# Masks of the decision trees by DMA in half of the blocks, and DRAM fills as planned steps, in a twelve-layer decoder kernel

## The chip, the cores and the metric

The kernel runs on one core of one Trainium2 chip. The metric is the device time of one execution in microseconds; the median of three runs of the kernel before is 2126.63 us (2123.84 to 2128.03).

## What is computed

64 sequences of 64 tokens, 128 wide, pass through four decoder layers of three sublayers each; every sublayer reads the layer norm of `x` and adds its result to `x`. The reference, cut to what matters here:

```python
x = x + _L0_attn_ref(_layernorm(x), ...)            # differential attention
x = x + _L0_xattn_ref(ctx_1024, _layernorm(x))      # alignment (dynamic time warping) with ctx
x = x + _L0_ffn_ref(_layernorm(x), ...)             # three trees (q, k, v), then attention over them
x = x + _L1_attn_ref(...); x = x + _L1_xattn_ref(...); x = x + _L1_ffn_ref(...)   # the last: experts
x = x + _L2_attn_ref(...); x = x + _L2_xattn_ref(...); x = x + _L2_ffn_ref(...)
x = x + _L3_attn_ref(...); x = x + _L3_xattn_ref(...); x = x + _L3_ffn_ref(...)   # the last: experts
# each tree of L0_ffn:
for _ in range(DEPTH):                              # 4 levels, 16 leaves
    score = jnp.einsum('nd,nd->n', xf, node_w[cur]) + node_b[cur]
    cur = 2 * cur + 1 + (score >= 0)
sel = jax.nn.one_hot(cur - N_NODES, N_LEAVES)
hidden_all = jax.nn.relu(jnp.einsum('nd,ldh->lnh', xf, w1) + b1[:, None, :])      # 64 wide per leaf
hidden = hidden_all * sel.T[:, :, None]
out = jnp.einsum('lnh,lho->no', hidden, w2) + sel @ b2
```

All leaves are computed for all tokens, and those that a token did not choose are masked.

## The kernel before

The 4096 tokens are 8 blocks of 512 (`NB`, `BT`), four tiles of 128 tokens each; `x` stays in SBUF for the whole run.

**Order of the work.** The program has five stages: a setup, the first flow (`front_group`: L0, L1 up to the router of its experts), the pages of L1's experts (`L1_ffn`), the last flow (`L2_group`: L2 and L3 up to the router), and L3's experts (`L3_ffn`). In a flow, every step is given to a planner (`Flow.add`) with its engine and a cost in microseconds, the steps that it follows, the buffers that it takes and frees, and a `tail`: the time after its end until its result counts as there (a DMA's landing). `Flow.play` plays the steps on a model of the five engines and the buffer rings: always the one that can begin first, ties by rank, which is a number of its group (layer and block) less the longest way that is left behind it. `ORDERS` holds these numbers for the two flows, one for each group in the order in which the groups are added; if the count fits, they are the start, and 300 variations of them are played. The best play's order is then emitted, and each engine runs its instructions in just that order. SP (SyncE) issues all plain DMAs of the flows, in order, as one queue. Instructions of the setup lie outside that order: the framework places them by their dependencies and their place in the program.

**The setup** loads `x`, the constants and the weights of L0's attention. `run` (L2594 on) clears a zero tile `z`, a part of `r`, the table of the alignment (`dt_r`). `setup_L3_ffn` (L2483, L2484) writes it to the 8 experts' ranges of `moe_x` and to the spare rows of the output, `setup_L1_ffn` (L2111) to 8 ranges of `pages`: 17 fills of DRAM, 660 KB most of them. `open_L0_ffn` (L1691, L1693) loads the trees' two matrices, q, k and v, 512 KB each; then follow 23 small loads (L1046, L1701).

**First flow.** L0's attention runs block by block; DVE takes each score's maximum (L546) and subtracts it (L555). The alignment works on two halves of the blocks (`ALIGN`: 0 to 3, 4 to 7): each block's distances (`L0_dist`: its load `ld` of ctx at L1476 and L1478, squares on ACT at L1483), then for all four blocks a root, a store to DRAM, a border written into `r` (`bd`, POOL), a load back (L1562), a chain of 64 row scans on DVE (L1571), masks, and 64 scans backwards (L1633); a store, and per block a product with ctx (L1671). The trees of a block (`flow_L0_ffn`) wait for that.

**The trees.** For each of three trees `m` and four pairs `pr` of two leaves' columns: an up step (`u`, PE), two matmuls with `w1` (L1770) and two with a leaf table `f0_em` (L1772) that add -2^100 to the columns of leaves not chosen, taken from `notT` (one less the transposed choice); a ReLU with the bias (`r`), on ACT (L1781) or DVE (L1783), which makes the masked columns zero; a down step (`d`, PE) with `w2` (L1797, or L1807 for the third tree), at the last pair also with `b2` and the choice. The two PSUM pairs `mm`, three `hT` buffers (ring H) and two places `dnq` limit how many steps are open. The ring G has 18 buffers of 2 KB per partition for nearly everything else.

**Where things meet.** A router (`f1`, `f3`) norms `x` (`norm_parts`, with `hold` for steps to wait for), chooses experts and scatters rows by GpSimd (L894). In the last flow, a step `("out", blk)` stores `x` to the output before the router norms it in place.

Of the kernel before, what the change touches and what calls it, by code (L numbers as in the profile page):

```python
# [13 lines left out]
F32 = mybir.dt.float32  # L14
# [24 lines left out]
    "G": (512, "xn xT qT kT o oT sq sqT sT cn cT d2 iv mn up selT qk va f0e f0p rxT x1hn x1hid x1hT x1qT x1s x1pT x1ht x1z ycT yk yv yw "  # L39
# [3 lines left out]
    "A": (1024, "a2g"), "nT": (BT // 2, "nT"),  # L43
# [9 lines left out]
            mk=3, pb=1, nT=2, sel=2, dnq=2, H=3, f0b=3)  # L53

ALIGN = (((0, 1, 2, 3), 0), ((4, 5, 6, 7), 64))
CH = 8
# [11 lines left out]
        -78, -130, -17, 83, 425, 288, 115, 418, -33, 78, -134, -156, 215, -90, 682, 1069,  # L68
        303, 144, -1217, 183, 789, -13, 984, 583, 481, 437, 284, 311, -1038, 373, 195, 674,
        712, 393, 386, 668, -42, 541, 336, 716, 395, 991, 806, 438, 608, 426, 954, 7,  # L70
        1467, 1071, 1229, 1113, 735, 436, 169, 809, 1278, -142, 384, -48, 197, -359, -463, -65,
        1393, 119, 168,
    ),
    "last": (
        73, 34, 202, 80, 99, 97, 99, 104, 237, 223, 166, 253, 232, 275, 304, 249,
        120, -51, 133, 224, 273, 279, 293, 300, 182, 260, 272, 280, 460, 443, 297, 421,
        240, 294, 248, 291, 283, 227, 312, 426, 324, 285, 380, 385, 224, 524, 526, 513,
        428, 588, 339, 442, 724, 441, 631, 469, 499, 576, 363, 568, 530, 473, 594, 609,
# [949 lines left out]
class Decoder:  # L1028
    def __init__(self, ctx, tc, ins, out):
        self.tc, self.nc, self.ins, self.out = tc, tc.nc, ins, out  # L1030
        self.base = self.const = ctx.enter_context(tc.tile_pool(name="const", bufs=1))
        self.small = ctx.enter_context(tc.tile_pool(name="small", bufs=4))
        self.dram = ctx.enter_context(tc.tile_pool(name="scratch", bufs=1, space=DRAM))
        self.psum = ctx.enter_context(tc.tile_pool(name="psum", bufs=1, space=PSUM))
        self.now, self.owed, self.turns = {}, {}, {"ps": 0, "mm": 0}
        self.flip = 0
        self.route1 = None
        self.half = None

# [202 lines left out]
    def loaded(self, fl):  # L1242

        key = ("loads", 0, "in")
        if key not in fl.keys:
            fl.add(key, {"SP": .1}, lambda e: None, tail=80.0)
        return key

    def front_group(self, layers):

        with ExitStack() as ctx:
# [4 lines left out]
            def parts(pools_ctx, pools, fl):  # L1256
                x = [None] * NB
                if "L0_ffn" in layers:
                    self.open_L0_ffn(pools_ctx)
# [12 lines left out]
                if "L0_ffn" in layers:  # L1272
                    x = [self.flow_L0_ffn(fl, blk, x[blk]) for blk in range(NB)]
# [15 lines left out]
                if r is not None:  # L1289
                    for blk in range(NB):  # L1290
                        r.flow(fl, blk, x[blk], hold=self.aligned)
                    self.flow_shared(fl, r)
# [3 lines left out]
            self.attend(parts, G=18, B=6, lg=1, rt=1)  # L1296
# [163 lines left out]
    def flow_L0_xattn(self, fl, blks, p0, x):  # L1460
# [98 lines left out]
        add("bd", {"POOL": .5}, border, [("L0_dist", blks[-1], "bn")])  # L1559
# [125 lines left out]
    def open_L0_ffn(self, ctx):  # L1685
        nc, ins = self.nc, self.ins
        one = self.f0 = self.pool(ctx, "f0", 1)
        self.f0_w1 = one.tile([P, 3, 8, P], F32, name="w1")
        self.f0_w2 = one.tile([P, 3, 8, D], F32, name="w2")
        for m, k in enumerate("qkv"):  # L1690
            nc.sync.dma_start(self.f0_w1[:, m].rearrange("p c f -> p (c f)").rearrange("p (l h) -> p l h", h=64),  # L1691
                              ins[f"L0_ffn_{k}_w1"].rearrange("l d h -> d l h"))
            nc.sync.dma_start(self.f0_w2[:, m], ins[f"L0_ffn_{k}_w2"].rearrange("(c p) o -> p c o", p=P))  # L1693
        self.f0_b1 = self.load("f0_b1", ins["L0_ffn_b1T"], [P, 3, 8], pool=one)
        self.f0_nw = self.load("f0_nw", ins["L0_ffn_node_wT"], [P, 45], pool=one)
        self.f0_nb = self.load("f0_nb", ins["L0_ffn_node_b"].partition_broadcast(P), [P, 45], pool=one)
        self.f0_em = self.load("f0_em", ins["c_leaf"], [96, 8, P], BF16, pool=one)
        self.f0_b2 = one.tile([96, D], F32, name="b2")
        nc.gpsimd.memset(self.f0_b2, 0.0)
        for m, k in enumerate("qkv"):  # L1700
            nc.sync.dma_start(self.f0_b2[32 * m : 32 * m + 16, :], ins[f"L0_ffn_{k}_b2"])  # L1701
        self.f0_sel = [one.tile([P, TB, 3, 32], F32, name=f"sel{i}") for i in range(2)]
        for t in self.f0_sel:
            nc.gpsimd.memset(t, 0.0)

    def flow_L0_ffn(self, fl, blk, x):
        nc, one, c = self.nc, self.f0, self.c
        w1, w2, em, b2 = self.f0_w1, self.f0_w2, self.f0_em, self.f0_b2
# [43 lines left out]
        def leaves_out(e):  # L1752
            tp = self.flat(st.pop("tp"))[:96]
            st["selT"] = self.sb("selT")[:96]
            st["notT"] = self.sb("nT", (P, BT), BF16)[:96]
            if e is nc.scalar:
                nc.scalar.copy(st["selT"], tp)
                nc.scalar.activation(st["notT"], tp, AF.Identity, bias=self.ones[:96, 0:1], scale=-1.0)
            else:
                nc.vector.tensor_copy(st["selT"], tp)  # L1760
                nc.vector.tensor_scalar(st["notT"], tp, -1.0, 1.0, ALU.mult, ALU.add)

        def up(m, pr):
            k = slice(32 * m, 32 * m + 16)

            def f(e):
                st["hT", m, pr] = self.sb("hT", (P, 2, BT))
                ps = st["up", m, pr] = self.pair()
                for i in range(2):
                    nc.tensor.matmul(ps[:, i], w1[:, m, 2 * pr + i, :], st["xT"], start=True, stop=False)  # L1770
                for i in range(2):
                    nc.tensor.matmul(ps[:, i], em[k, 2 * pr + i, :], st["notT"][k], start=False, stop=True)  # L1772
            return f

        def relu(m, pr):
            def f(e):
                ps, hT = st.pop(("up", m, pr)), st["hT", m, pr]
                for i in range(2):
                    b = self.f0_b1[:, m, 2 * pr + i : 2 * pr + i + 1]
                    if e is nc.scalar:  # L1780
                        nc.scalar.activation(hT[:, i], ps[:, i], AF.Relu, bias=b)  # L1781
                    else:
                        nc.vector.tensor_scalar(hT[:, i], ps[:, i], b, 0.0, ALU.add, ALU.max)  # L1783
            return f

        def down(m, pr):
            k = slice(32 * m, 32 * m + 16)

            def f(e):
# [3 lines left out]
                ps, hT = st["dn", m], st.pop(("hT", m, pr))  # L1793
                last = pr == 3
# [5 lines left out]
                else:  # L1800
                    if pr == 0:

                        nc.tensor.matmul(ps, self.onesb[0:1, :], em[0:1, 1:5, :].rearrange("p c f -> p (c f)"), start=True, stop=False)
# [60 lines left out]
        add("lv", {"PE": .55}, leaves, ["dc"], [("tp", "lv", 1), ("selT", "selT", 3), ("nT", "nT", 12)], [("sel", "sel")])  # L1864
        add("lo", {"ACT": 1.15, "DVE": 1.35}, leaves_out, ["lv"], [], [("tp", "lv")])
        for m in range(3):
            for pr in range(4):
                add(f"u{m}{pr}", {"PE": 2.35}, up(m, pr), ["xT", "lo"] + ([f"u{m}{pr-1}"] if pr else []), [("mm", f"u{m}{pr}", 1), ("hT", f"h{m}{pr}", 1)] + ([] if pr else [("dnq", f"d{m}", 1)]),
                    [("xT", "xT"), ("nT", "nT")])
                add(f"r{m}{pr}", {"ACT": 1.4, "DVE": 1.5}, relu(m, pr), [f"u{m}{pr}"], [], [("mm", f"u{m}{pr}")])  # L1870
                add(f"d{m}{pr}", {"PE": 1.75 + (pr == 3) * (.86 if m < 2 else .5)}, down(m, pr),
                    [f"r{m}{pr}"] + ([f"d{m}{pr-1}"] if pr else []),
# [231 lines left out]
    def setup_L1_ffn(self):  # L2104
# [3 lines left out]
        for i in range(0, PAGES, CAP // PAGE):  # L2108
            rows = slice(i * PAGE, min(i + CAP // PAGE, PAGES) * PAGE)
            n = (rows.stop - rows.start) // P  # L2110
            self.nc.sync.dma_start(self.pages[rows, :].rearrange("(t p) d -> p t d", p=P), self.zero[:, 0:n])  # L2111
# [365 lines left out]
    def setup_L3_ffn(self):  # L2477


        self.xg = self.dram.tile([NE * CAP + 2 * NT * P, XROW], F32, name="moe_x")  # L2480
        z = self.zero
        for e in range(NE):
            self.nc.sync.dma_start(self.xg[e * CAP : (e + 1) * CAP, :].rearrange("(c p) d -> p c d", p=P), z)  # L2483
        self.nc.sync.dma_start(self.out[NSEQ * S :, :].rearrange("(c p) d -> p c d", p=P), z[:, :, 0:D])  # L2484

    def L2_group(self, layers):

        with ExitStack() as ctx:
# [10 lines left out]
            def parts(pools_ctx, pools, fl):  # L2499
# [18 lines left out]
                if r is not None:  # L2518
                    for blk in range(NB):
                        fl.add(("out", blk), {"SP": .1}, (lambda b: lambda e: self.nc.sync.dma_start(outb[b], self.x[b]))(blk), [x[blk]])  # L2520
# [254 lines left out]
```

## Time and profile before

| | before |
|---|---|
| median of 3 runs | 2126.63 us |
| the profiled execution | 2125.41 us |
| its span, first to last instruction | 2123.6 us |
| granted TensorE clock, mean | 0.912 |
| busy: PE, PEld, DVE, ACT, POOL | 1834, 1245, 1293, 1078, 880 us |
| first flow: first alignment, first tree matmul (L1770), last | 181 to 288, 317.9, 899 us |
| pages of L1's experts | from about 1085 to 1247 us |
| last flow, then L3's experts | from about 1250, from about 1927 us |

In lists of groups a row gives line, engine, operation, output and input, shapes and count, then busy us and the mean ns of one, then the idle time before them and what ended it. A row of the waits gives the total in us, the times and the longest. In timelines a row gives the start, the time, the engine and the line; `SPq` is the issue of a DMA by SP's queue. A row of the DMA view gives the KB of one and the median us from issue to landing. An f32 matmul shows as two records.

### The profile page before, as it was taken

The numbers are of one execution on the slowest core, as the hardware profiler recorded it, in microseconds if no ns is written. First come the engines' busy times: TensorE is split into PE (matmuls) and PEld (weight loads), VectorE is DVE, ScalarE is ACT, GpSimd is POOL, SyncE is SP. The second block draws the span as 40 slices with busy tenths as digits, with TensorE's granted clock in tenths as the row PEclk, the third lists the DMA queues.
The fourth block names the chain that finished last, engine by engine and source line by source line (L and its number), as shares of the span: only waits on it lengthen the run. The fifth ranks groups of instructions, "written<-read, shape, count | busy, mean of one in ns | idle before, by whom it ended". The sixth has DMA issues, their size and how long they took to land.

```text
span 2123.6 us, 42731 instructions
## 1 busy us (share of the span) xinstructions
PE 1834.1 (86%) x16748; PEld 1245.1 (59%) x16748; DVE 1293.3 (61%) x3683; ACT 1078.0 (51%) x2129; POOL 879.6 (41%) x1196
## 2 busy tenths in 40 slices
PE   7488559999999999998999966899999978936994
PEld 5366344453765554575778854567777756634763
DVE  7488982687574443388324336988988858751211
ACT  7386333443564533477234424776787755622431
POOL 8461215100232334024612247855463364255776
PEclk9798769999999999998899976999999978857998
DMA  9405410101010000010246631100000010024543
GB/s 256 114 22 158 140 46 21 22 20 23 8 37 11 11 21 21 1 50 27 80 116 208 209 109 55 36 21 17 26 22 7 22 56 21 13 66 89 93 68 29
DMA packets 160875, 125.97 MB, mean 59 GB/s; under 512 B 39057, under 2 KB 138690, under 8 KB 160674
## 3 DMA queue, kind: packets, MB, share of 16 engines
q1 hardware_dynamic: 137394, 82.04, 14.2%
q0 software_dynamic: 23280, 41.19, 7.8%
q8 instruction: 133, 2.18, 0.4%
q14 instruction: 68, 0.56, 0.1%
HBM read 75.40 MB, written 45.02 MB: 57 GB/s over the span
## 4 chain that ended last, share of the span: by engine, by line
PE 37%; POOL 10%; DVE 7%; issue 3%; ACT 3%; DMA 2%; SPq 0%; POOLq 0%; ACTq 0%; DVEq 0%
PE ps L1122 5%; POOL out_x L2582 4%; PE ps L590 4%; PE ps L2211 3%; PE mm L2203 3%; PE mm L525 2%; POOL moe_x L894 2%; PE mm L1770 2%; PE ps L2147 2%; POOL A L2273 1%; PE ps L415 1%; PE ps L1797 1%; PE mm L2438 1%; PE mm L2136 1%; PE mm L531 1%
## 5 line engine op out<-in xcount | busy, mean ns | idle before, releaser
L1122 PE MATMUL ps<-cpack,B 128*128 128x128 f32 x1280 | 184.7, 292 | 39.2 <-ACT G L428 25.1
L546 DVE TENSOR_REDUCE e<-mm 128x16 f32<-128x1024 f32 x160 | 191.7, 1218 | 35.8 <-PE mm L525 34.5
L576 ACT COPY B<-ps 128x512 f32<-128x512 f32 x320 | 171.4, 592 | 76.0 <-PE ps L1122 75.3
L1122 PEld LDWEIGHTS ps<-cpack,B 128*128 128x128 f32 x1280 | 153.9, 150 | 87.8 <-issue 26.4
L560 ACT ACTIVATE B<-B 128x1024 f32<-128x1024 f32 x160 | 166.3, 1057 | 67.6 <-DVE B L555 66.4
L1781 ACT ACTIVATE H<-mm,f_b 128x512 f32<-128x512 f32 x166 | 105.0, 683 | 176.3 <-PE mm L1772 174.8
L1132 POOL TENSOR_SCALAR rs_t<-ln_mv 128x4 f32<-128x4 f32 x88 | 19.2, 219 | 412.9 <-DVE ln_mv L1203 389.6
L590 PEld LDWEIGHTS ps<-vx,B 128*64 128x64 f32 x5120 | 167.4, 143 | 38.4 <-issue 12.1
L555 DVE TENSOR_TENSOR B<-mm,e 128x1024 f32<-128x1024 f32 x160 | 189.1, 1213 | 0.0
L1770 PE MATMUL mm<-G,w 128*128 128x512 f32 x384 | 185.4, 605 | 0.0
L590 PE MATMUL ps<-vx,B 128*64 128x18 f32 (+1 forms) x5120 | 179.6, 218 | 2.8 <-ACT B L576 1.1
L1122 PE MATMUL ps<-cpack,G 128*128 128x128 f32 x544 | 96.6, 301 | 82.6 <-ACT G L1223 36.8
L2582 POOL DMA_INDIRECT out_x<-ye,to x80 | 125.1, 1564 | 51.8 <-DVE ye L2580 27.5
L1122 PEld LDWEIGHTS ps<-cpack,G 128*128 128x128 f32 x544 | 66.6, 149 | 121.3 <-ACT G L1223 46.0
L525 PE MATMUL mm<-K,G 32*64 32x256 f32 x2560 | 104.9, 419 | 25.7 <-DVE B L555 23.8
L1223 ACT ACTIVATE G<-x,ln_sh,ln_rs 128x128 f32<-128x128 f32 x208 | 85.7, 487 | 71.9 <-POOL ln_sh L1217 71.9
L2204 ACT ACTIVATE hT<-mm,w 128x256 f32<-128x256 f32 x156 | 68.8, 474 | 104.3 <-PE mm L2203 104.3
L1797 PE MATMUL ps<-H,w 128*128 128x512 f32 x256 | 121.2, 607 | 0.0
L1770 PEld LDWEIGHTS mm<-G,w 128*128 128x128 f32 x384 | 66.7, 190 | 71.4 <-issue 69.8
L2570 ACT ACTIVATE hT<-mm,f_b 128x512 f32<-128x512 f32 (+1 forms) x96 | 58.9, 616 | 83.8 <-PE mm L2569 83.2
L1133 POOL TENSOR_TENSOR ln_rs<-rs_t,neghalf 128x4 f32<-128x4 f32 x88 | 92.9, 1056 | 7.2
L2576 PEld LDWEIGHTS ps<-w,hT 128*128 128x128 f32 x640 | 81.4, 191 | 18.8 <-issue 13.4
(423 smaller groups left out, 4004.1 us busy)
## 6 DMA issues: line engine op xcount, KB each, us to landing
ahead_L_xattn_k<-G SPq DMA_DIRECT2D x24, 256.0 KB, 2.7
moe_x<-r SPq DMA_DIRECT2D x8, 660.0 KB, 9.4
xe<-moe_x SPq DMA_DIRECT2D x8, 660.0 KB, 5.1
xe<-pages SPq DMA_DIRECT2D x39, 132.0 KB, 2.4
paged<-ye SPq DMA_DIRECT2D x39, 128.0 KB, 1.9
pages<-r SPq DMA_DIRECT2D x7, 660.0 KB, 10.6
G<-in_ctx SPq DMA_DIRECT2D x16, 256.0 KB, 3.0
G<-in_ctxT SPq DMA_DIRECT2D x16, 256.0 KB, 3.7
```

The source lines that it names most:

```text
L525: nc.tensor.matmul(banks[g][b * S : (b + 1) * S, pr * 256 : (pr + 1) * 256], qT[rows, at : at + S], kx[rows, :, at : at + S], start=plain ...
L546: nc.vector.tensor_reduce(mx, sc.rearrange("p g (r k) -> p (g r) k", k=S), AX.X, ALU.max)
L555: nc.vector.tensor_tensor(ex, sv, d.bc(st["mx", u].unsqueeze(2), [P, 16, S]), ALU.subtract)
L560: nc.scalar.activation(st["ex", u], st["ex", u], AF.Exp)
L576: (nc.scalar.copy if e is nc.scalar else nc.vector.tensor_copy)(st["pT", u][:, gi], st.pop(("pt", u, gi)))
L590: nc.tensor.matmul(av[b * S : (b + 1) * S, pr, 2 * gi + jp], pT[:, gi, 2 * pr + jp, b * S : (b + 1) * S], v[:, (2 * dp + pr) * 2 + b, 2 * ...
L1122: self.nc.tensor.transpose(t[:cols, i, :], src[:, i, :], self.ident)
L1133: self.nc.gpsimd.tensor_tensor(dst, t, self.neghalf[:, :n], ALU.pow)
L1770: nc.tensor.matmul(ps[:, i], w1[:, m, 2 * pr + i, :], st["xT"], start=True, stop=False)
L1781: nc.scalar.activation(hT[:, i], ps[:, i], AF.Relu, bias=b)
L1797: nc.tensor.matmul(ps, w2[:, m, 2 * pr + i, :], hT[:, i], start=(pr + i == 0), stop=False)
L2582: d = nc.gpsimd.indirect_dma_start(self.out[:, :], bass.IndirectOffsetOnAxis(ap=to[:, r0 + i : r0 + i + 1], axis=0), ye[:, r0 + i, :], Non ...
```

## The change

1. The 17 fills are no longer issued by the setup but are collected in `self.fills`, and become steps `("fill", 0, i)` of the first flow, 3.6 us of SP each; the alignment's border and L1's router wait for all of them. The trees' matrices become three steps `("L0_trees", m, "w")`, 5.6 us of SP each. The other loads count as there 45 us after the start of the plan, not 80.
2. In blocks 4 to 7 (`FOLD`) the up step has no mask matmuls. The transposed choice is also written as bf16 and stored to DRAM (`put`); for each pair two DMAs load the rows of its leaves, each repeated over 64 partitions (`masks`), into one of two buffers of a new ring `fm`, a load being allowed once the up step two before is done (`AHEAD`). The ReLU is one DVE operation, `max(ps, -b1) * mask`, which leaves out the bias; what is missing, `b1 @ w2` of the chosen leaf, is computed once by a small product (`flow_L0_bias`) and added to `b2`.
3. The ring G has 17 buffers in the first flow.
4. In the last flow the store of `x` has a tail of 4.4 us.
5. `ORDERS`: 72 new numbers for the first flow (67 before), 12 of 64 changed in the last.

```diff
+AHEAD = 2
+FOLD = ((False,) * 3,) * 4 + ((True,) * 3,) * 4
...
-            fl.add(key, {"SP": .1}, lambda e: None, tail=80.0)
+            fl.add(key, {"SP": .1}, lambda e: None, tail=45.0)
...
-                        r.flow(fl, blk, x[blk], hold=self.aligned)
+                        r.flow(fl, blk, x[blk], hold=self.aligned + self.filled)
...
-            self.attend(parts, G=18, B=6, lg=1, rt=1)
+            self.attend(parts, G=17, B=6, lg=1, rt=1)
...
-        add("bd", {"POOL": .5}, border, [("L0_dist", blks[-1], "bn")])
+        add("bd", {"POOL": .5}, border, [("L0_dist", blks[-1], "bn")] + self.filled)
...
+            fl.add(("L0_trees", m, "w"), {"SP": 5.6}, weights, tail=2.4)
...
+        add("B", {"POOL": 3.0}, spread, [self.loaded(fl)] + [("L0_trees", m, "w") for m in range(3)], [("f0B", "B", 1)])
+        add("pr", {"PE": 3.0}, product, ["B"], [("tp", "ps", 1)], [("f0B", "B")])
+        add("b2", {"DVE": .5}, plus, ["pr"], [], [("tp", "ps")])
...
+        def put(e):
+            nc.sync.dma_start(rows, st.pop("leaf"))
+
+        def masks(m, pr):
+
+            def f(e):
+                t = st["mask", m, pr] = self.sb("f0m", (P, 2, BT), BF16)
+                at = 32 * m + 4 * pr
+                src = rows[at : at + 4].rearrange("(i h) t -> h i t", h=2)
+                for h in range(2):
+                    nc.sync.dma_start(t[h * S : (h + 1) * S], src[h].partition_broadcast(S))
+            return f
...
-                    nc.tensor.matmul(ps[:, i], w1[:, m, 2 * pr + i, :], st["xT"], start=True, stop=False)
-                for i in range(2):
-                    nc.tensor.matmul(ps[:, i], em[k, 2 * pr + i, :], st["notT"][k], start=False, stop=True)
+                    nc.tensor.matmul(ps[:, i], w1[:, m, 2 * pr + i, :], st["xT"], start=True, stop=fold[m])
+                for i in range(0 if fold[m] else 2):
+                    nc.tensor.matmul(ps[:, i], self.f0_em[k, 2 * pr + i, :], st["notT"][k], start=False, stop=True)
...
+                    nc.vector.scalar_tensor_tensor(hT[:, i], ps[:, i], self.f0_nb1[:, m, ch : ch + 1], st["mask", m, pr][:, i], ALU.max, ALU.mult)
...
+        if any(fold):
+            add("st", {"SP": .7}, put, ["lo"], [], [("f0l", "leaf")], tail=2.6)
...
+                was = order.index(n) - AHEAD if fold[m] else -1
+                if fold[m]:
+                    add(f"k{m}{pr}", {"SP": 1.3}, masks(m, pr), ["st"] + ([f"u{order[was] // 4}{order[was] % 4}"] if was >= 0 else []),
+                        [("f0m", f"k{m}{pr}", 1)], tail=3.0)
...
-            self.nc.sync.dma_start(self.pages[rows, :].rearrange("(t p) d -> p t d", p=P), self.zero[:, 0:n])
+            self.fills.append((self.pages[i * PAGE : min(i + CAP // PAGE, PAGES) * PAGE, :], XROW))
+
+    def flow_fills(self, fl):
+
+        self.filled = []
+        for i, (rows, n) in enumerate(self.fills):
+            c = rows.shape[0] // P
+            f = lambda e, rows=rows, n=n, c=c: self.nc.sync.dma_start(rows.rearrange("(c p) d -> p c d", p=P), self.zero[:, 0:c, 0:n])
+            fl.add(("fill", 0, i), {"SP": 3.6}, f)
+            self.filled.append(("fill", 0, i))
...
-            self.nc.sync.dma_start(self.xg[e * CAP : (e + 1) * CAP, :].rearrange("(c p) d -> p c d", p=P), z)
-        self.nc.sync.dma_start(self.out[NSEQ * S :, :].rearrange("(c p) d -> p c d", p=P), z[:, :, 0:D])
+            self.fills.append((self.xg[e * CAP : (e + 1) * CAP, :], XROW))
+        self.fills.append((self.out[NSEQ * S :, :], D))
...
-                        fl.add(("out", blk), {"SP": .1}, (lambda b: lambda e: self.nc.sync.dma_start(outb[b], self.x[b]))(blk), [x[blk]])
+                        fl.add(("out", blk), {"SP": .1}, (lambda b: lambda e: self.nc.sync.dma_start(outb[b], self.x[b]))(blk), [x[blk]], tail=4.4)
```

## The prediction

> **What bounds the kernel now.** I read the table of windows first, because the program is a row of stages with different limits.
>
> ```profile
> core 0: us, PE busy (x) PEld busy (x) DVE busy (x) ACT busy (x) POOL busy (x), PEclk, DMA share, GB/s
> 0.00:50.00 50.00, 36.63 (x527) 25.41 (x528) 37.20 (x114) 37.08 (x64) 40.82 (x82) 1.00 1.03 256
> 50.00:100.00 50.00, 22.66 (x308) 17.47 (x308) 21.19 (x40) 18.79 (x44) 22.21 (x18) 0.72 0.55 136
> ...
> 200.00:250.00 50.00, 35.15 (x500) 21.20 (x496) 45.16 (x152) 22.67 (x36) 5.37 (x6) 0.88 0.57 199
> 250.00:300.00 50.00, 17.69 (x195) 12.97 (x196) 43.90 (x149) 11.70 (x26) 7.07 (x9) 0.53 0.15 36
> ...
> 350.00:400.00 50.00, 50.00 (x279) 28.57 (x278) 22.09 (x64) 22.68 (x50) 11.70 (x19) 1.00 0.03 8
> ...
> 800.00:850.00 50.00, 50.00 (x198) 24.98 (x197) 16.38 (x74) 17.66 (x37) 22.12 (x32) 1.00 0.07 23
> ```
>
> The columns are busy us (and counts) of PE, PEld, DVE, ACT and POOL. Three things: in 50 to 100 every engine is idle more than half the time, just behind 50 us in which the DMA engines are full; to 318 DVE is the busiest engine (247.7 us against PE's 212.6: attention, then the first alignment); from 300 to 950 PE is busy 644.4 of 650 us, and it is the bound. Then I asked who waited in 40 to 200, and what SP's queue issued there.
>
> ```profile
> ACT G L1483 <- DMA G<-in_ctx: 26.5, 1, 26.5
> PE ps L1122 <- ACT G L428: 25.1, 1, 25.1
> DVE bqs L332 <- DMA L_attn_bq_c<-in_L_attn_bq: 13.5, 1, 13.5
> ```
>
> ```profile
> 14.61 16.85 SPq L2483 DMA_DIRECT2D moe_x<-r  x8
> 31.50 2.35 SPq L2484 DMA_DIRECT2D out_x<-r  x1
> 33.89 20.48 SPq L2111 DMA_DIRECT2D pages<-r  x8
> ...
> 70.77 0.43 SPq L1046 DMA_DIRECT2D L_attn_bk_c<-in_L_attn_bk  x1
> ...
> 76.90 0.39 SPq L1476 DMA_DIRECT2D G<-in_ctx  x1
> ```
>
> SP issues in order. The 17 fills hold it for 39.7 us (16.85 + 2.35 + 20.48), the trees' matrices to 65.9, and 23 small loads (0.47 each) to 76.8; the first load of ctx comes at 76.9. ACT's squares (L1483) wait for it, ACT's later work (L428) is queued behind, and PE stands from 58.3 to 83.4. DVE loses 13.5 and 12.5 us there. As DVE's work up to the end of the alignment (288) decides when the trees' matmuls can begin, these 25 us move everything behind them.
>
> The third look is PE's timeline in the trees:
>
> ```profile
> 800.63 1.88 PE L1770 MATMUL mm<-G,w 128*128 128x512 f32 x4
> 802.44 0.60 PE L1772 MATMUL mm<-nT,f_em 16*128 16x512 bf16 x2
> 802.97 1.98 PE L1770 MATMUL mm<-G,w 128*128 128x512 f32 x4
> 804.89 0.60 PE L1772 MATMUL mm<-nT,f_em 16*128 16x512 bf16 x2
> ```
>
> The mask's two matmuls hold PE for 0.53 us (802.44 to 802.97) of each up step.
>
> **The change part by part, against the profiled execution (2125.41 us, span 2123.6; the median of three is 2126.63, 1.2 more).**
>
> *Fills and tree matrices become planned steps.* Nothing is removed: the same 17 fills and 6 matrix loads pass through SP, but behind the 23 small loads, and between planned ctx loads. The bq load, issued at 70.4 before, should come by about 20 (10.6 + 23 x 0.47 = 21.5), so DVE's 13.5 us wait ends. Ctx loads now stand among the fills: the planner lets SP take a fill of 3.6 us whenever it is free, so by ranks two of the first four blocks' ctx loads pass some fills and two come last. Real fills take 39.7 / 17 = 2.3 us, but start at about 24 (21.5 and one matrix pair), and a load behind them lands as late as they do (9.4 us, row below). After one matrix pair and 8 fills the planner is at 5.6 + 8 x 3.6 = 34 and has ctx at 38; the chip is at 24 + 8 x 2.3 = 42 and has it at 52, while ACT, some 7 us behind the plan (x is there at 6.6), wants it at 45. That is 7 us of a new wait of the same kind, 9 with the load's second half, and 0 if other work stands ahead; as ACT runs in order I take 6. Gain: 25.1 - 6 = 19 (16 to 25). The border (POOL, `bd`) now waits for the fills, and the layer norms' roots are queued behind it on POOL; but the fills end near 70, and the alignment's load was issued at 172.9. The trees' matrices are wanted after 270. If DVE had cover for the wait, the gain would be nothing; its idle 13.5 and 12.5 us say it has none.
>
> *Masks by DMA in blocks 4 to 7.* PE loses 48 x 0.53 = 25.4 us in the stage it bounds. It gains 24 small products for the bias (as L1807: 32 records in 3.84 us are 16 products, so 0.24 each): 5.8 us, or nothing if they fall into PE's gaps before 290 (21.7 and 17.8 us long); I take 2. ReLU of these blocks is now one DVE operation, max and multiply; the nearest row has the same shape, PSUM source and kind:
>
> ```profile
> L2364 DVE SCALAR_TENSOR_TENSOR G<-ps,cpack,Q 128x512 f32<-128x512 f32 x16 | 11.9, 742 | 4.9 <-PE ps L2360 4.8
> L1781 ACT ACTIVATE H<-mm,f_b 128x512 f32<-128x512 f32 x166 | 105.0, 683 | 176.3 <-PE mm L1772 174.8 <-issue 1.3
> ```
>
> 96 x 0.742 = 71 us on DVE, where half of the old 26 (0.746 each, 10 us) go away; ACT loses some 57 us, which gains nothing, since it waits 175 us for PE here. DVE is busy 217 of 400 us in 550 to 950; with 61 more it is at 70%, so PE's other blocks cover it; where a ReLU stands behind a pair of attention reductions (2.4 us) PE may wait: bounds 0 and 12, I take 3.
>
> The mask loads: 96 of 128 KB, 0.62 us of SP each. Nearest rows:
>
> ```profile
> H<-in_ctx SPq DMA_DIRECT2D x16, 128.0 KB, 3.0
> moe_x<-r SPq DMA_DIRECT2D x8, 660.0 KB, 9.4
> ```
>
> A step (up and down) is 3.8 us of PE without masks; with two buffers a mask may be issued when the ReLU two steps before has ended, and has 2 x 3.8 - 1.5 = 6.1 us; it takes 1.24 + 3.0 = 4.2. Hidden, with 1.9 us to spare; behind a mask load that waits for its buffer, SP holds only path and context loads in 520 to 950. Behind a ReLU that waits for its mask stand DVE's attention reductions, and the step's down matmul waits for it. 12.6 MB over 400 us is 32 GB/s beside the 21 moved there. The leaf store and first mask (some 7 us a block) delay the first ReLU, while PE has another block's attention. Gain: 25.4 - 2 - 3 = 20 (0 to 25).
>
> Here the Trainium skill speaks against the edit (DMA: Bandwidth & Descriptors, "Rules for kernel authors"): two transfers to disjoint partition halves serialize, and one of 128 partitions is better. The masks come in two such halves. The H rows are also two halves, issued 0.6 us apart, each 3.0 us to landing, so this trace doesn't show it; by the page the sum would come to about 2114, as the rival below works out from rows.
>
> *The rest.* One G buffer less (17 of 18), the loads' due time 80 to 45, all 72 ranks of the first flow and 12 of the last new, and 4.4 us for the store of x (measured 2.3). No row prices a reordering. In the first flow PE is idle 105 us before 318, so a better order can gain, and a worse one lose: 0, bounds 15 either way. In the last flow no wait of any size names the store, and its stages stay: 0, bounds 6.
>
> Sum: 2125.4 - 19 - 20 = 2086, or **2087** as a median.
>
> **Rivals.**
> - *The start stall moves* (SP's fills ahead of a ctx load that ACT needs, as now): the fills' 9.4 us landing and in-order ACT speak for it, the small loads' earlier place against. Masks alone: 2087 + 19 = 2106. Chance 0.13.
> - *The mask wait eats PE's gain* (landing about 5.7 us, or DVE late by 0.4 us a step): 2087 + 20 = 2107. Chance 0.12.
> - *The two halves run one after the other*: landing 6.0, so 1.24 + 6.0 - 6.1 = 1.1 us late in each of 24 pairs of steps, 27 us: 2114. Chance 0.04, as the H rows speak against it. (This is the rule of the Trainium skill's page above.)
> - *Slower*: the mask's landing becomes the pace of the folded trees. If a load that repeats its rows over 64 partitions takes 9.4 us, as the fills do, each pair of steps loses 1.24 + 9.4 - 6.1 = 4.5 us, 109 in all: 2196. It turns the sign when it eats 39 us, 1.6 a pair: a landing over 3.0 + 1.9 + 1.6 = 6.5 us. For it: SP runs in order, so one load that waits for its buffer holds the next (the eight `mk` loads of the second alignment took SP from 453.9 to 496). Against: the 3.0 us rows; `pb`, read back behind its store, lands in 2.6; and late in the run a bias repeated over 128 partitions (512 KB) lands in 3.7. 0.20, with whatever part of it PE can fill with other blocks, so mostly 2131 to 2170.
> - *The planner does not use the new ranks* if their number differs from the groups. I count 1 + 3 + 8 + 8 + 2 + 8 + 1 + 1 + 8 + 8 + 8 + 8 + 8 = 72; they fit; if not, both gains stay and its own order costs up to the 15 above, 2102. Chance 0.01.
>
> **The numbers.** The forecast holds 0.50. The low end is its own: both gains whole (-11) and the orders' best (-21) and some idle PE before the trees refilled: 2045. The high end takes in the single-gain cases and the mild part of the slower one: 2140. A measurement tells 0.2% (4 us) from no change. Faster: 0.50 + 0.13 + 0.12 + 0.04, less 0.03 where a bad order eats a single gain: 0.76. Within: 0.04. Slower: 0.20.
>
> **What would show it.** Right: no idle of PE over 12 us before 100; the first alignment scan (L1570) near 162, not 181; the first tree matmul near 298; PE full until about 910; 96 mask matmuls, not 192; the masked ReLU at 0.74 us, waiting for PE and not for a DMA; mask loads landing in about 3 us. Wrong: a ReLU that waits for the mask load, which costs from 6.1 us on; an ACT wait for ctx of over 12 us; or a first flow whose PE is no longer full.

## The result, and the profile after

The changed kernel takes 2109.47 us (median of 8 runs, 2104.5 to 2117.14) where the kernel before takes 2123.96 beside it (8 runs): a ratio of 0.9934, with a 95% interval of 0.9916 to 0.9951. It is faster by about 14 us; the forecast was 39.6. The profiled execution takes 2111.14 us, its span 2109.4. Below, kernels are compared by their ratio to the kernel before, run beside them; a thousandth is 2.1 us. The first four experiments ran on a chip on which the kernel before took 2166.2 us, 1.9% longer; there only the ratios count.

The table of windows, same columns as before (busy us of PE, PEld, DVE, ACT and POOL, granted clock, DMA share, GB/s):

```profile
0.00:50.00 50.00, 35.10 (x524) 24.28 (x524) 36.97 (x114) 36.62 (x64) 40.90 (x82) 1.00 0.91 221
50.00:100.00 50.00, 43.79 (x716) 34.15 (x716) 42.69 (x87) 40.74 (x93) 38.07 (x38) 0.97 0.73 183
200.00:250.00 50.00, 16.56 (x260) 11.41 (x260) 43.91 (x161) 10.84 (x21) 4.05 (x4) 0.71 0.27 90
...
350.00:400.00 50.00, 47.08 (x482) 29.24 (x481) 39.83 (x110) 34.22 (x69) 8.15 (x15) 0.97 0.13 24
800.00:850.00 50.00, 50.00 (x367) 32.36 (x367) 28.88 (x61) 13.27 (x28) 8.90 (x18) 1.00 0.19 56
```

The hole behind the fills is gone: in 50 to 100 PE is busy 43.8 us, not 22.7. But in 350 to 400, where PE was busy 50.0 of 50 us, it now has 47.1: the stage that PE bounds is no longer quite full.

SP's queue at the start (start, duration, line, what it moves):

```profile
23.09 18.41 SPq L2194 DMA_DIRECT2D moe_x<-r  x8
41.54 3.04 SPq L2194 DMA_DIRECT2D out_x<-r  x1
44.63 21.23 SPq L2194 DMA_DIRECT2D pages<-r  x8
66.04 2.01 SPq L1481 DMA_DIRECT2D G<-in_ctx  x1
```

The small loads (21 by the profile, not 23) are through by 21.3, and then, behind one pair of the trees' matrices, all 17 fills pass in one piece: 42.7 us. The first ctx load comes at 66.0, only 11 us earlier than before, yet no wait for it stands among ACT's longest up to 120 (7.1 us at most, for PE): the new order gives ACT other work, and it is busy 40.7 of the 50 us from 50 to 100. The first alignment scan starts at 152.6 (181.0 before), the first tree matmul at 292.8 (317.9).

PE in the trees, and the two kinds of ReLU by group (the columns of a group: busy us, mean ns of one, then the idle time ahead of them and who ended it):

```profile
799.78 1.98 PE L1833 MATMUL mm<-G,w 128*128 128x512 f32 x4
801.60 1.04 PE L1125 MATMUL ps<-cpack,B 128*128 128x128 f32 x8
802.47 1.88 PE L1833 MATMUL mm<-G,w 128*128 128x512 f32 x4
```

```profile
L1850 DVE SCALAR_TENSOR_TENSOR H<-mm,nb,fm 128x512 f32<-128x512 f32 x96 | 66.9, 742 | 47.4 <-PE mm L1833 46.4 <-PE ps L1125 0.9
L1846 ACT ACTIVATE H<-mm,f_b 128x512 f32<-128x512 f32 x90 | 56.9, 684 | 98.0 <-PE mm L1835 98.0
```

```profile
fm<-leaf SPq DMA_DIRECT2D x96, 128.0 KB, 3.0
```

The up matmuls stand without mask matmuls behind them (96 of those are left, on the line that ACT's ReLU waits for); the masked ReLU takes 0.742 us and waits for PE, not for its mask, which lands in 3.0 us. So every part does what it says, and single operations and transfers take the time that was forecast. The last tree matmul starts at 881.2 (899.5 before), the first page at 1067.2 (1083.3), and from there to the end nothing changes (1042 us, 1040 before). Of the 25 us that the trees start earlier, 18 are left at their end and 16 at the first page, although PE has 27 us less to do: that is the question.

### The profile page after: what moved, and what is told of

The parts are those of the page before. It is cut to its first block, busy times and chain, and to the rows that moved or that the text cites. A ratio compares the mean times of both kernels' runs of the same rounds, so it can differ in the third digit from the quotient of the medians.

```text
span 2109.4 us, 42838 instructions
## 1 busy us (share of the span) xinstructions
PE 1808.1 (86%) x16700; PEld 1240.9 (59%) x16700; DVE 1338.3 (63%) x3738; ACT 1025.5 (49%) x2037; POOL 915.3 (43%) x1240
## 4 chain that ended last, share of the span: by engine, by line
PE 59%; DVE 14%; POOL 13%; issue 5%; ACT 4%; DMA 4%; SPq 0%; POOLq 0%; DVEq 0%; ACTq 0%
PE mm L1833 8%; PE ps L1125 7%; PE ps L1865 5%; PE ps L592 5%; POOL out_x L2666 4%; PE ps L2296 3%; PE mm L527 3%; PE mm L2288 3%; PE ps L1875 3%; DVE e L548 2%; POOL moe_x L896 2%; PE ps L417 2%; PE ps L2232 2%; DVE B L557 2%; POOL pages L896 2%
## 5 line engine op out<-in xcount | busy, mean ns | idle before, releaser
L578 ACT COPY B<-ps 128x512 f32<-128x512 f32 x320 | 171.4, 593 | 88.2 <-PE ps L1125 87.7
L592 PEld LDWEIGHTS ps<-vx,B 128*64 128x64 f32 x5120 | 164.0, 141 | 40.2 <-issue 13.1
L527 PEld LDWEIGHTS mm<-K,G 32*64 32x64 f32 x2560 | 53.9, 139 | 90.5 <-DVE B L557 64.4
L1226 ACT ACTIVATE G<-x,ln_sh,ln_rs 128x128 f32<-128x128 f32 x184 | 75.8, 488 | 62.6 <-POOL ln_sh L1220 62.5
L1846 ACT ACTIVATE H<-mm,f_b 128x512 f32<-128x512 f32 x90 | 56.9, 684 | 98.0 <-PE mm L1835 98.0
L1229 POOL TENSOR_SCALAR G<-x,ln_mv,ln_rs 128x128 f32<-128x128 f32 x104 | 84.2, 820 | 38.2 <-PE mm L1833 33.5
```

The source lines that it names most:

```text
L527: nc.tensor.matmul(banks[g][b * S : (b + 1) * S, pr * 256 : (pr + 1) * 256], qT[rows, at : at + S], kx[rows, :, at : at + S], start=plain ...
L578: (nc.scalar.copy if e is nc.scalar else nc.vector.tensor_copy)(st["pT", u][:, gi], st.pop(("pt", u, gi)))
L592: nc.tensor.matmul(av[b * S : (b + 1) * S, pr, 2 * gi + jp], pT[:, gi, 2 * pr + jp, b * S : (b + 1) * S], v[:, (2 * dp + pr) * 2 + b, 2 * ...
L1229: nc.gpsimd.tensor_scalar(xn[:, t, 0:D], xb[:, t, :], st["mv"][:, t, 0:1], st["rs"][:, t : t + 1], ALU.subtract, ALU.mult)
```

## The experiments

The theories at the start. A: what the start gains goes through to the end. B: PE pays part of it back. C: PE is the bound to 910 also with less work, so the mask matmuls are worth their 25 us. D: behind the last trees a chain of the last blocks becomes the bound. In the first experiments the planned order of the kernel *before* is kept to the step, and only what a step issues is edited, so that an edit and a reordering cannot be mixed up.

**Fills behind block 3's ctx, old order.**

```diff
  (load of L0_dist)  nc.sync.dma_start(st["cT"], ...)
+ if blk == 3:
+     for fill in self.fills + self.mats:   # 17 fills, 6 matrix loads
+         fill()
```

> The kernel before, with its planned order unchanged; only the 17 fills and the trees' 6 matrix loads are issued on SP behind the ctx loads of blocks 0 to 3 instead of at the start. Theory A (what the start gains goes through to the end): the first alignment scan comes 25 to 28 us earlier, and the whole falls by about 25 us, to 2099 (ratio 0.988). Rival B (PE, which is the bound from 300 on, has less of its other work done by then and pays the difference back): the scan comes 25 us earlier, but the whole falls by only 10 to 15 us, to about 2112.

Ratio 0.9941 (0.9924 to 0.9959): 12.5 us. The number looks like B, but the start itself gained only part of what was expected: the scan came at 165.9.

```profile
ACT G L1487 <- DMA G<-in_ctx: 20.5, 1, 20.5
```

This is the wait of the kernel before over again, some 60 us later (it ends at 140.1, before at 79.7): SP was held from 80 to 135, block 4's ctx load stood behind that, and ACT waited 20.5 us for it. This run shows that the stall can move (a rival of the prediction); it does not decide between A and B.

**No mask matmuls in blocks 4 to 7, old order** (the mask of these blocks is left out).

```diff
- nc.tensor.matmul(..., start=True, stop=False)
- for i in range(2):
+ nc.tensor.matmul(..., start=True, stop=blk >= 4)
+ for i in range(0 if blk >= 4 else 2):
      nc.tensor.matmul(ps[:, i], em[k, 2 * pr + i, :], st["notT"][k], ...)
```

> The kernel before, with its planned order unchanged; the mask's matmuls of blocks 4 to 7 are left out (and with them the mask of these blocks), so PE has 48 x 0.53 = 25 us less to do in the trees, and nothing takes their place. Theory C (PE is the bound until 910 also with less work, as the prediction had it): about -25 us, 2099. Rival D (behind the last trees the last blocks' attention and router steps form a chain of their own that becomes the bound): 0 to -10 us, 2114 to 2124, with the last tree matmul 20 us earlier and PE idle 10 to 20 us more between it and the first page.

Ratio 0.9879 (0.9862 to 0.9897): 26 us, as C has it (25), and more than D's 0 to 10: in the old order PE's saving reaches the end.

**Both.**

> Both of the two edits before at once, in the old planned order. If the two gains add as the prediction added them (A and C): -50 us, 2074. If the start's gain passes and PE's saving is lost behind the trees (A and D): -25 to -33, 2091 to 2099. If the start's gain is paid back too (B and D): -10 to -22.

Ratio 0.983 (0.9812 to 0.9848): 36 us, close to the sum of the two (12.5 + 26 = 38). The gains add.

**After, without the mask loads** (a constant mask).

```diff
- for h in range(2):
-     nc.sync.dma_start(t[h * S : (h + 1) * S], src[h].partition_broadcast(S))
+ st["mask", m, pr] = <one constant tile>
```

> The kernel after, with its planned order unchanged; the 96 mask loads are not issued, and the masked ReLU multiplies by a constant tile (so the masks of blocks 4 to 7 are left out). If the mask loads cost nothing (they land in 3.0 us and the ReLU waits for PE): the time of after, 2109 within 4 us. If they cost the missing gain: 2085 to 2095.

Ratio 0.9918 (0.9902 to 0.9934) against 0.9934 with them, on another chip: 3 us, inside the intervals. The loads are not where the gain went.

**Fills spread over the ctx loads of blocks 0, 1 and 2, old order.**

```diff
- if blk == 3: ...
+ for fill in {0: fills[:4], 1: fills[4:9], 2: fills[9:], 3: mats}.get(blk, ()):
+     fill()
```

> The kernel before, planned order unchanged; the fills are issued behind the ctx loads of blocks 0 (4 of them), 1 (5) and 2 (8), the trees' matrices behind that of block 3, so that no ctx load stands behind all of them. In the run that issued them all behind block 3's, ACT waited 20.5 us for block 4's ctx, and the first tree matmul came only 13 to 17 us earlier than before. Theory A (what the start gains goes through to the end): no ACT wait for ctx over 5 us, the first tree matmul 24 to 27 us earlier than before, ratio 0.987 to 0.989. Rival B (part is paid back while PE is the bound): the same start, ratio 0.993 or more.

Ratio 0.9866 (0.9846 to 0.9886): 28.5 us. ACT has no wait for ctx among its longest; the scan starts at 154.3, the first tree matmul at 291.8, the last at 874.7, the first page at 1059.9: 26, 25 and 23 us earlier than before. The ratio lies just past A's range and far from B's: A holds, B falls. One part of the change, in the old order, gives twice what the whole change gives.

**No mask matmuls, and ReLU of these blocks on DVE, old order** (constant in place of the mask).

```diff
+ if blk >= 4:
+     nc.vector.scalar_tensor_tensor(hT[:, i], ps[:, i], b, <constant>, ALU.max, ALU.mult)
```

> The kernel before, planned order unchanged, without the mask's matmuls of blocks 4 to 7 (as the run that left them out, ratio 0.988), and now with the ReLU of these blocks on DVE alone, in the form of the change (max and multiply, with a constant in the place of the mask). Theory E (DVE's 96 x 0.74 us are covered by PE's work; the new order is what lost PE's 25 us): ratio 0.987 to 0.991. Rival F (DVE becomes late for attention, and PE waits for it): back to 0.995 or more.

Ratio 0.9932 (0.9916 to 0.9948), between the two ranges. Read against 0.9879 it leaves 11 us for DVE, in the direction of F; but the two ran on different chips, so the run without DVE was repeated later.

**After, without mask loads, and every second folded ReLU on ACT** (constant mask, none on ACT).

> The kernel after, planned order unchanged, without mask loads (constant mask, as the run that left them out, ratio 0.992), and with every second folded ReLU on ACT (0.68 us, plain ReLU): DVE has 36 us less in the trees. If DVE's load is what holds PE up in after's order (F): ratio 0.985 or less, and the trees' stage at least 12 us shorter. If it is the order itself (E): 0.990 to 0.993.

Ratio 0.992 (0.9905 to 0.9935), as with all of them on DVE (0.9918, on another chip). In the new order 36 us less of DVE's work gain nothing, so DVE's load is not what holds PE up there: E, the order, remains.

**The whole masks in the old order, fills spread.** Leaf store, mask loads (three buffers in the `mk` tiles that the second alignment has left), bias product, DVE's masked ReLU: all of the change's work, hung into the old steps by hand.

```diff
  (leaves_out)  + nc.vector.tensor_copy / nc.scalar.copy(leaf, tp)
                + nc.sync.dma_start(self.f0_leaf[96 * blk : 96 * blk + 96, :], leaf)
                + <issue mask loads while a buffer is free>
  (up)          - mask matmuls
  (relu)        + nc.vector.scalar_tensor_tensor(hT[:, i], ps[:, i], nb1, mask[:, i], ALU.max, ALU.mult)
                + <free the buffer, issue the next mask load>
  (down)        + b2f in the place of b2
```

> The kernel before, planned order unchanged, with the fills spread behind the ctx loads (alone: ratio 0.987) and the whole of the masks by DMA of blocks 4 to 7, loads, bias product and DVE's masked ReLU, put into the old order by hand (three mask buffers in tiles that the second alignment has left). Same work on PE as after. Theory E (the masks are worth 12 to 20 us here, and after's new order loses 20 us or more): 0.978 to 0.982, 2079 to 2087, the first page at 1040 to 1048. Rival G (the masks themselves are worth nothing in whole: loads, DVE and bias eat what PE saves): 0.986 to 0.989.

Ratio 0.9816 (0.9792 to 0.9839), 2082.16 us beside 2124.21: 39 us by the ratio, in theory E's range, within 5 us of the time that was forecast for the change, and faster than both kernels. So the parts are worth together what the prediction said (two misses cancel in that, see below), and after's order loses (0.9934 - 0.9816) x 2125 = 25 us for the same work. "Order" stands here for all in which the two kernels still differ: the ranks, 17 G buffers for 18, two mask buffers for three, and the places of the fills.

**The converse: the work of before in after's order.** Mask matmuls back on PE, plain ReLU on ACT, no leaf store, no mask loads.

> The converse: the kernel after, in its own planned order and with its early start, but with the work of before in blocks 4 to 7 (mask matmuls on PE, plain ReLU on ACT, no leaf store and no mask loads). The kernel with the fills spread does the same work in the old order (0.987). Theory E: the new order loses 20 us or more against it, so 0.997 or more. Rival G (the order costs nothing): 0.985 to 0.990.

Ratio 1.0086 (1.0067 to 1.0105), as theory E has it: slower than before in spite of its early start; the kernel with the fills spread has the same PE work, but for the bias product that this run still computes (some 6 us of PE by the prediction's row), at 0.9866. With this work the new order costs 47 us. It was planned for less PE, so this is an upper case; the sign is not in doubt. The run shows one thing more: against it, the change in the same order is 1.0086 - 0.9934 = 0.0152 faster, 32 us. So in the new order, too, PE's saving reaches the end.

**No mask matmuls again, beside the others.**

> Again the kernel before without the mask's matmuls of blocks 4 to 7 and nothing in their place, now beside the others on one chip. On another chip it gave 0.988; with DVE's ReLU added, on this kind of chip, 0.993. If DVE's ReLU costs 11 us: 0.988 again. If what differs is the chip: 0.992 to 0.994.

Ratio 0.9895 (0.9877 to 0.9914), 22 us.

**Fills spread, no mask matmuls, ReLU on DVE, old order** (constant mask).

> The fills spread, no mask matmuls in blocks 4 to 7, ReLU of these blocks on DVE with a constant: the run with the masks in the old order less its mask loads, leaf stores and bias product. If the two gains add: 0.987 - 0.007 = 0.980. What lies between this run and the one with the masks is the price of loads, stores and bias: 0 to 4 us expected.

Ratio 0.9805 (0.9785 to 0.9825). Spread fills and missing matmuls alone would add to 0.9866 - 0.0105 = 0.9761, so DVE's ReLU costs 0.0044, some 9 us (8 by 0.9932 less 0.9895, each to within some 5 or more, by the intervals); and loads, stores and bias together cost 0.9816 - 0.9805 = 0.0011, some 2 us, which the intervals do not tell from nothing.

What was open then: is it the numbers, or the 18th G buffer that the new order gave up? Both runs keep the changed kernel and take 72 numbers from a longer search with the planner's own costs.

**18 G buffers again** (mask buffers in the `mk` tiles).

```diff
- self.attend(parts, G=17, B=6, lg=1, rt=1)
+ self.attend(parts, G=18, B=6, lg=1, rt=1)   # and other numbers in ORDERS["first"]
```

> The kernel after with 18 G buffers again (the two mask buffers lie in tiles that the second alignment has left), and with 72 numbers from a longer search for this ring. The planner's own end of the first flow is 976.2, against 986.2 after. If the 17th ring was what the new order lost (theory R): ratio 0.981 to 0.987, near the masks in the old order. If a planned order loses some 20 us on the chip against the old one whatever its ring (theory N): 0.988 to 0.994.

Ratio 0.9862 (0.984 to 0.9884): 29 us faster than before, 15 us better than the change, and in theory R's range.

**17 buffers, other numbers.**

> The kernel after with 17 G buffers as it is and only other numbers, from an equally long search; the planner's own end is 981.0, against 986.2. Theory R: the ring stays, so 0.990 to 0.994 (5 us at most from the plan). If the numbers alone were poor: 0.986 or less. If the planner's end says little about the chip: anything, also above 0.994.

Ratio 0.9891 (0.9871 to 0.9911): 23 us, 9 better than the change; it lies between the range of R and that of poor numbers. So of the 25 us some 9 (to within 6, by the intervals) were the numbers alone. The next 6 (0.9891 - 0.9862, at the edge of the intervals) lie between two runs that differ in the ring and in their numbers, so they aren't shown to be the ring's. The last 10 (0.9862 - 0.9816) neither run wins back: a newly planned order with 18 buffers is still that much behind the old one with the parts hung into it. That other numbers give another time also shows that the planner did use its 72 numbers, which settles the last rival.

## Why the prediction was wrong

Where the new order loses is seen in the three stages: to the first tree matmul, to the last, to the first page. Rows of windows (PE busy is the second figure behind the stretch), first of the kernel before:

```profile
0.00:318.00 318.00, 212.63 (x3001) 157.48 (x3001) 247.69 (x711) 173.38 (x338) 132.11 (x179) 0.81 0.45 122
318.00:900.00 582.00, 580.00 (x3436) 311.31 (x3434) 313.95 (x1016) 265.51 (x529) 140.39 (x219) 1.00 0.07 18
900.00:1083.00 183.00, 171.36 (x1539) 126.10 (x1538) 111.33 (x337) 96.34 (x192) 69.78 (x115) 0.93 0.17 51
```

of the change:

```profile
0.00:292.00 292.00, 201.03 (x3006) 147.24 (x3008) 246.97 (x709) 174.71 (x345) 147.41 (x202) 0.87 0.49 133
292.00:881.00 589.00, 577.95 (x3738) 331.07 (x3736) 383.99 (x1129) 235.96 (x487) 161.35 (x250) 0.99 0.15 42
881.00:1067.00 186.00, 157.52 (x1188) 111.18 (x1187) 87.01 (x281) 73.69 (x138) 68.02 (x101) 0.85 0.14 44
```

and of the whole masks in the old order:

```profile
0.00:289.00 289.00, 205.14 (x2988) 150.16 (x2990) 247.69 (x711) 172.92 (x337) 131.74 (x179) 0.85 0.50 135
289.00:861.00 572.00, 557.55 (x3407) 314.51 (x3404) 364.03 (x1094) 218.35 (x455) 141.70 (x224) 0.99 0.14 41
861.00:1046.00 185.00, 173.01 (x1538) 126.55 (x1536) 112.98 (x340) 95.56 (x191) 70.59 (x117) 0.92 0.16 50
```

PE's work sums to 964.0, 936.5 and 935.7 us: the change does save its 27 us. PE's idle time (stretch less busy) is 105 + 2 + 12 = 119 before, 91 + 11 + 28 = 130 after, 84 + 14 + 12 = 110 in the old order with the same work. So after's order has 20 us more of idle PE: 7 ahead of the trees, 3 less in them, and 16 behind them. There it pulled 14 us of PE's work (171.4 less 157.5) into the trees, but the stretch stayed as long, 186 us (183 before). This goes with the order and not with the work: with the mask matmuls back on PE, the new order's idle time is 89 + 8 + 27, and that of the old one, fills spread, 82 + 2 + 12. PE's waits behind the trees, of the change:

```profile
966.14 1.64 PE L1125 MATMUL ps<-cpack,G 128*128 128x128 f32 x4 [6.69 <-ACT G L2085]
979.73 1.63 PE L1125 MATMUL ps<-cpack,r 128*128 128x128 f32 x4 [9.16 <-ACT r L1226]
```

of the run with the work of before in the same new order:

```profile
998.33 1.64 PE L1125 MATMUL ps<-cpack,G 128*128 128x128 f32 x4 [6.71 <-ACT G L2092]
1011.93 1.63 PE L1125 MATMUL ps<-cpack,r 128*128 128x128 f32 x4 [9.17 <-ACT r L1226]
```

and of the old order with the work of the change:

```profile
954.90 1.63 PE L1123 MATMUL ps<-cpack,G 128*128 128x128 f32 x4 [3.58 <-ACT G L2064]
960.48 1.63 PE L1123 MATMUL ps<-cpack,r 128*128 128x128 f32 x4 [1.30 <-ACT r L1224]
```

The same two steps (softmax of the cross attention, a norm) cost 15.9 us of idle PE in the new order, with either work, and 4.9 in the old one. As I read the timeline, the new order has nothing left to run beside them; no run of its own takes these two waits away, so this reason is argued and not shown. In both runs with other numbers PE is also idle longer behind the last tree, 25 us with 17 buffers (179 less 154.4) and 23 with 18 (164 less 141.1), against 12 in the old order. For the run with 18 buffers that is about the 10 us by which it stays behind, as it is idle 4 us more ahead of the trees and 5 less in them; why is open. No new order tried here keeps the time behind the trees as full as the old one.

**The start** (gain 19, from 25.1 less a new wait of 6): the mechanism was right, the term too small. The new wait did not come, neither in the change nor with the fills spread in the old order; alone the part measured 28.5 us (0.9866). The forecast of the first scan (162) and of the first tree matmul (298) were late by 9 and 5 us for the same reason. That the stall could move was a rival, and the first experiment shows it at 20.5 us when a ctx load stands behind all fills.

**The masks** (gain 20, from 25.4 - 2 - 3): right in kind, too large. PE's matmuls were worth 22 us, DVE's ReLU cost 9, where I took 3 between bounds of 0 and 12, and the rest about 2; in the old order the whole came to (0.9866 - 0.9816) x 2125 = 11 us. I worked DVE out at 70% busy in this stretch and took that for cover. The start came out 9.5 too small and the masks 9 too large, so that their sum, 39 in the forecast and 39 in the old order, is right by luck.

**The mask's landing**: the 3.0 us and the spare time held, so the slower rival (6.5 us and more) and that of halves one after the other fall. Of the rival in which waits eat PE's gain, the landing falls too; DVE late was real, but at 9 us in 48 steps, 0.2 each, half of what it needed. The Trainium skill's rule that two transfers to disjoint partition halves serialize (DMA: Bandwidth & Descriptors, "Rules for kernel authors") decided nothing here: two halves issued 0.6 us apart landed in 3.0 us each, and taking all 96 loads away gave 3 us, within the intervals. No run here compares a pair of halves with one whole load.

**The rest** (0, bounds 15 either way): this is the step that failed. "0, bounds 15" stood for all 72 ranks and for one buffer less, no row priced it, and it measured 25 us lost, past its own bound. With this the sum is -28.5 - 11 + 25 = -14.5; measured -14. It closes by construction, as the 25 is what the change lacks against the run in the old order; the converse run is the independent sign that the new order loses. In place of "0" the runs show idle PE: 20 us more, most of it behind the last tree. "PE full until about 910" was listed as a sign to watch, and it came out wrong: PE is idle 11 us between the first and the last tree matmul (2 before), and much longer behind that: from 950 to 1000, where it was busy 42.4 of 50 us, it is now busy 30.6. The first paragraph of the prediction had read "it is the bound" from the old order, which keeps PE full until its last tree and nearly full behind it, and carried that to the new one. But the saving itself did not stop counting, as it would by theory D: with the mask matmuls the new order's trees take 621 us from first to last, without them 588, and the stretch behind them 186 both times. What is lost is idle time that the new order has with either work.

## What to carry to other kernels

When a change brings a new order with it, the order is a part of the change with a price of its own, and here not a small term: hang the new work into the old order and the old work into the new one, and the prices come apart (11 us of masks, 28 of fills, 25 lost to the order). "Engine X is the bound from here to there" holds for the order in which it was read; in a new order, look at that engine's idle time stage by stage, behind the stage that it bounds above all. When a long block of transfers is moved, the load behind it inherits the stall: spread it over gaps of its queue, as in the old order here, or see that the waiting engine has other work, as in the new one.

## What was not expected of the hardware

The fills hold SP for less time when they come in groups: 42.7 us in one piece after the change, 39.7 before, 40.2 behind block 3's ctx load, and 7.80 + 2.68 + 6.92 + 17.95 = 35.4 us in groups (5, 4 and 8 in this trace) with ctx loads between them. The two other runs with spread fills show 34.1 and 34.5.

DVE's load cost PE time though DVE was far from full. In the old order without mask matmuls, PE is idle 5.5 us in the trees with the ReLU shared by ACT and DVE (556.0 us less 550.5), and 11.7 with all ReLUs of these blocks on DVE (567.6 less 555.9), though DVE is then busy only 364 of 568 us. In the old order with the whole masks the masked ReLUs themselves sat 42.9 us idle for PE. So an engine can wait for PE in many of its steps and still make PE late in others. Of PE's waits there only 3 us name the ReLU (two times); the longest, 7.5 us, is for one norm on ACT, and no run shows whether DVE's load is behind that.
